# Layer 1's expert blocks in interleaved thirds of their table, and reads of an expert's matrix with a condition

## The chip, the core and the metric

The kernel runs on one core of one Trainium2 chip. The metric is the device time of one execution in microseconds (us); lower is better. A core has a matrix engine (PE, whose weight loads the profile lists apart as PEld), VectorE (DVE), ScalarE (ACT), GpSimd (POOL) and SyncE (SP). Each works through its own instructions in order, and they wait for one another by semaphores. Data moves between the chip's main memory and the on-chip buffers by DMA; in this kernel SP and POOL issue the DMAs.

## The reference, cut to what matters

Four layers follow one another on 2708 rows of 256 numbers. Each adds to its input the result of a graph step (a product with the 2708 x 2708 adjacency matrix, weighted in a different way in each layer) and then that of a feed-forward step. The change touches the feed-forward step of layer 1, in which every row goes to one of eight experts:

```python
H = jax.nn.gelu(xf @ W1 + b1, approximate=False)          # 2708 x 1024
probs = jax.nn.softmax((H @ Wg + bg) / TEMP, axis=-1)     # 2708 x 8
assign = jnp.argmax(probs, axis=-1)
out = jnp.zeros_like(xf)
for e in range(Wd.shape[0]):
    y = H @ Wd[e] + bd[e]                                 # Wd[e] is 1024 x 256
    sel = (assign == e)[:, None]
    out = out + jnp.where(sel, probs[:, e:e + 1] * y, 0.0)
```

## The kernel before, in words

The layers run one after the other, with their edges overlapped. In the feed-forward step of layer 1 the kernel computes H for every row (`hidden`, line 363, called from `send1`, line 1098), writes it to main memory (`hid`), and routes: `route` (line 377) gives every row a place behind the other rows of its expert, and a scatter on POOL (`scatter`, line 502) writes the row's number and its factor to that place in the table `taken`. This is done for three groups of rows (line 30): tiles 0 to 7, 8 to 15 and 16 to 21, a tile being 128 rows.

The experts' products then run by blocks of at most 128 rows of one expert. `blocks` (line 415) works out two tables at run time. The first has NA = 9 blocks that are full after two groups (2048 rows), in order of expert (`full`, line 1325). The second, `rest`, has what remains after all rows are routed, in order of expert too; its first ALWAYS = 15 blocks always run (line 1330), and any further ones stand in a branch (`run_rest`, line 624) that is taken only if there are more. For each block the table says which expert it belongs to (`ei`) and where its rows stand in `taken` (`ix`).

The class `Units` (line 630) does a block in these steps:

- `fetch_names` (line 645): POOL gathers the numbers and factors of the block's rows from `taken` into `names`.
- `fetch_rows` (line 655): POOL gathers the rows of H from `hid` into one of four buffers `hs`, 512 KB.
- `fetch` (line 547): SP loads the block's expert number into a register (`expert_of`, line 530), and `weights1` (line 1052) issues the read of that expert's matrix and bias, 128 rows of 9216 bytes, into one of three buffers `wb`. It waits until the last reader of the buffer, the addition in line 720 three blocks earlier, is done.
- `turn` (line 665): PE transposes the rows (line 670), ScalarE copies them out (line 671).
- the product (line 719): 16 matmul instructions in the profile, into one of two accumulators `yacc`; VectorE adds the bias (line 720) and multiplies by the factor (line 721) into one of two buffers `ys`.
- `scatter` (lines 723 and 505): POOL writes the block's rows to `given` in main memory.

`more` (line 681) keeps names, rows and matrices some blocks ahead. `begin` (line 674) is called in line 1262 with the nine blocks of the first table, before the last group is routed, and `add` (line 690) in line 1332 with the fifteen of the second. `pieces` (line 701) is a generator: its first five steps are taken between parts of the last group's gating in `send1` (lines 1178 to 1189), the others in line 1333. `beside` (line 1206) adds, at blocks given by number, constants of layer 2: the products of line 245 and some small reads on POOL. Layer 2 begins with a read of `given` (line 1406) that waits for every scatter into it. The order of instructions on each engine comes from the compiler's scheduler where it isn't fixed by hand.

Of the kernel before, what the change touches and what calls it, by code (L numbers as in the profile page):

```python
# [8 lines left out]
F32 = mybir.dt.float32  # L9
# [6 lines left out]
P = 128  # L16
N = 2708
D = 256
# [18 lines left out]
def rows(t):  # L37
    return min(P, N - t * P)
# [28 lines left out]
def adj_ffn4(ctx: ExitStack, tc: tile.TileContext, a: dict, out: bass.AP):  # L67
    nc = tc.nc
# [78 lines left out]
    def after(i, past):  # L147

        tc.add_manual_dep(i.ins, past, mybir.DependencyInfo(
            mybir.DependencyClass.NoSync, mybir.DependencyReason.DATA), reason="order")  # L150
# [137 lines left out]
    def spread_out(values):  # L288

        n = values.shape[1]  # L290
        p = ps_tmp()
        for z in range(0, P, Q):
            te.matmul(p[z : z + Q, :n], lhsT=ident[:LAST, :Q], rhs=values[:LAST, :], start=True,
                      stop=True, tile_position=(0, z))
        s.copy(values, p[:, :n])

    def last_rows(dst, parts, filler):

        filler.memset(dst, 1.0)
        for q, k, c0, w in parts:  # L300
            nc.sync.dma_start(dst[q * Q : q * Q + LAST, k : k + w],
                              a["adjT"][FULL * P :, c0 : c0 + w])
# [6 lines left out]
    def by_turns(own):  # L309

        return [(n, t, k) for z in range(2) for n, (t, k, _) in enumerate(own) if n % 2 == z]

    def last_columns(dst):

        v.memset(dst[:, FULL, :], 1.0)
        nc.sync.dma_start(dst[:, :FULL, :], a["adjT"][: FULL * P, N - Q :].rearrange(
            "(t p) c -> p t c", p=P))
        for z in range(0, P, Q):
            nc.sync.dma_start(dst[z : z + LAST, FULL, :], a["adjT"][FULL * P :, N - Q :])
# [445 lines left out]
    taken = [tc.dram_tile([2 * N, XW], F32, name="taken0"), tc.dram_tile([N, 2], F32, name="taken1")]  # L765
# [10 lines left out]
    held = sum(rows(t) for q in GROUPS[:-1] for t in q)  # L776


    NA, MOST = 9, (2 * N + E * (P - 1)) // (2 * P)
# [4 lines left out]
    ALWAYS, HALVES = 13, 2  # L784
    with ExitStack() as l0:
# [15 lines left out]
        hcs, reads, own_rows = [], [], []  # L801
# [87 lines left out]
        for tiles in GROUPS:  # L889
# [8 lines left out]
            for j in range(FULL):  # L898
                r = rows(j)
                ad = gp.tile([P, GMAX * P], F32, name="adrow", bufs=5)[:r, :w]  # L900
                i = nc.sync.dma_start(ad, a["adjT"][j * P : j * P + r, c0 : c0 + w])
# [22 lines left out]
                for p, pair in zip(acc, pairs):  # L924
                    for n in pair:
                        if n == len(own):
                            continue
                        _, k, q = own[n]
# [12 lines left out]
                if end and j == 0:  # L941
                    items = [(early, b, past0, taken[0][: 2 * held0], True) for b in range(N0)]
# [4 lines left out]
                if end and j == NT - 5:  # L947
                    past = list(scattered["taken0"])
# [22 lines left out]
            if tiles is GROUPS[-2]:  # L971
                full = blocks(hw, tp, known, NA - N0, 2 * P, "A", done=early[2], full=True)
        rest = blocks(hw, hc, known, MOST - NA, 2 * P, "B", done=full[2], least=P)
# [9 lines left out]
        past = list(scattered["taken0"])  # L983
        rest = [(rest, b, past, taken[0], False) for b in range(MOST - NA)]
# [37 lines left out]
        for q, t0, t1 in ((P, 0, FULL), (LAST, FULL, NT)):  # L1022
            d = ps_tmp()
            for t in range(t0, t1):
                i = te.matmul(d[:q, t : t + 1], lhsT=cs[:, t * P : t * P + q], rhs=ones,
                              start=(t == t0), stop=(t == t1 - 1))
# [13 lines left out]
    held = sum(rows(t) for q in GROUPS1[:-1] for t in q)  # L1040
    NA, MOST = 9, (N - E) // P + E + 1
    assert NA <= -(-(held - E * (P - 1)) // P)
    ALWAYS = 15
    with ExitStack() as l1:
# [2 lines left out]
        b1 = tp.tile([P, HC], F32, name="b1")  # L1047
        g.dma_start(b1, a["L1_ffn_b1"])
        hw = l1.enter_context(tc.tile_pool(name="h1", side="right", reuse_waits="tile", bufs=1))
        wbs, reads = {}, []  # L1050

        def weights1(b, e):
            wb = wbs["pool"].tile([P, 2048 + D], F32, name="wb", bufs=3)
            i = nc.sync.dma_start(wb, a["L1_ffn_Wdp"][bass.ds(e, 1)].rearrange("e p n -> p (e n)"))
            after(i, reads[-1])
            return wb.rearrange("p (f d) -> p f d", d=D)

# [148 lines left out]
        def beside(b):  # L1206
            if b == NA + 9:
                work1.at_end = scattered["given1"][-1].name
            if b == NA + 4:
# [8 lines left out]
                for i in nc.cur_bb.bb.instructions[first:]:  # L1218
                    if i.engine in (mybir.EngineType.DVE, mybir.EngineType.PE):
                        tc.add_manual_dep(i, work1.last, mybir.DependencyInfo(  # L1220
                            mybir.DependencyClass.NoSync, mybir.DependencyReason.DATA),
                            reason="order")

        work1 = Units(hw, given[1], weights1, hid)
        for tiles in GROUPS1:
            end = tiles is GROUPS1[-1]
# [15 lines left out]
            for j in [*range(12), FULL, *range(12, FULL)]:  # L1242
                r = rows(j)
                if j == FULL:

                    r = P
                    if tiles is GROUPS1[0]:
                        spread_out(sup[:, FULL, :])
                ad = gp.tile([P, 8 * P], F32, name="adrow", tag="adrow", bufs=4)[:r, :w]
                if j < FULL:  # L1250
                    i = nc.sync.dma_start(ad, a["adjT"][j * P : j * P + r, c0 : c0 + w])
                    reads.append(i.ins.name)
                else:
                    last_rows(ad, [(q, 0, c0, w) for q in range(P // Q)], v)
                v.tensor_scalar(mask[:r, j, c0 : c0 + w], ad, 0.0, None, op0=ALU.is_gt)  # L1255
                for t, k, q in own:
                    if t == j:
                        v.tensor_tensor(ad[:, k : k + r], ad[:, k : k + r], ident[:r, :r], ALU.add)  # L1258
                        v.tensor_scalar(diag[:r, j, :r], ad[:, k : k + r], 0.0, None, op0=ALU.is_gt)
                if end and j == NT - 5:  # L1260
                    past = list(scattered["taken1"])
                    work1.begin([(full, b, past, taken[1][:held], True) for b in range(NA)])
                if end and j == 2:
                    cols = gp.tile([P, 8 * P], F32, name="adlast", tag="adrow", bufs=4)[
                        :, : NT * Q].rearrange("p (t c) -> p t c", c=Q)
                    last_columns(cols)
                    v.tensor_scalar(mask[:, :FULL, FULL * P :], cols[:, :FULL, SKIP:], 0.0, None,
                                    op0=ALU.is_gt)
                    own_cols = cols[:, FULL, SKIP:]
                    v.tensor_scalar(mask[:, FULL, FULL * P :], own_cols, 0.0, None, op0=ALU.is_gt)  # L1270
                    v.tensor_tensor(own_cols, own_cols, fold[:, :LAST], ALU.add)
                    v.tensor_scalar(diag[:, FULL, :LAST], own_cols, 0.0, None, op0=ALU.is_gt)
                    last = last_sums(acc[-1].rearrange("p k d -> p (k d)"), cols,
                                     lambda j, r: sup[:r, j, :], D)
                    grow(last[:, None, :], FULL, 1, LAST)
                if j == FULL:
                    for n, t, k in by_turns(own):
                        last_product(acc[n // 2][:, n % 2, :], n // 2, ad, k, sup[:, FULL, :],
                                     False)
                    continue  # L1280
                kept_rows.append((j, ad))
                if end and FULL - 4 < j < FULL - 1:
                    continue
                for p, pair in zip(acc, pairs):
                    for jj, ad in kept_rows:
                        for n in pair:
                            if n == len(own):
                                continue
                            _, k, q = own[n]
                            te.matmul(p[:q, n - pair[0], :], lhsT=ad[:, k : k + q],  # L1290
                                      rhs=sup[:, jj, :], start=(jj == 0 and n == pair[0]),
                                      stop=(jj == FULL - 1 and n == pair[-1]))
                kept_rows.clear()
# [30 lines left out]
            if tiles is GROUPS1[-2]:  # L1324
                full = blocks(hw, gt, known, NA, P, "A", full=True)
        rest = blocks(hw, gt, known, MOST - NA, P, "B", done=full[2])
        too_many = count_left(hw, (rest[2], ALWAYS))
        gate.close()
        past = list(scattered["taken1"])
        items = [(rest, b, past, taken[1], False) for b in range(ALWAYS)]  # L1330
        more = [(rest, b, past, taken[1], False) for b in range(ALWAYS, MOST - NA)]
        work1.add(items)
        for _ in between:
            pass
        work1.run_rest(hc, more, left[0])


# [24 lines left out]
    with tc.tile_pool(name="t3", reuse_waits="tile", bufs=1) as t3:  # L1362
# [34 lines left out]
        with tc.tile_pool(name="g2", reuse_waits="tile", bufs=1) as gp:  # L1397
# [5 lines left out]
            for tiles in FOURS:  # L1403
                n, t0 = len(tiles), tiles[0]
# [3 lines left out]
                for k in range(0, n, 2):  # L1408
                    for q, m in (((P, 2),) if rows(t0 + k + 1) == P else
                                 ((P, 1), (rows(t0 + k + 1), 1))):  # L1410
                        i = k if q == P else k + 1
# [66 lines left out]
            p = ps_tmp()  # L1478
# [7 lines left out]
            for n in (5, 5, 5, 4, 2):  # L1486
# [4 lines left out]
                for j in range(NT):  # L1491
                    r = P
                    e = gp.tile([P, 5 * P], F32, name="e", bufs=4)
                    i = v.scalar_tensor_tensor(e[:r, :w], Rb[:r, c0 : c0 + w], G[:r, j, :],  # L1494
                                           mask[:r, j, c0 : c0 + w], op0=ALU.max, op1=ALU.mult)
# [51 lines left out]
            p = ps_tmp()  # L1547
# [68 lines left out]
        rest = N - len(stretches) * WIDE  # L1616
# [25 lines left out]
        with tc.tile_pool(name="h2", reuse_waits="tile", bufs=2) as hp:  # L1642
# [26 lines left out]
            p = ps_tmp()  # L1669
# [3 lines left out]
            p = ps_tmp()  # L1673
# [86 lines left out]
            was = None  # L1760

            parts = CHUNKS[:-2] + [(CHUNKS[-2][0], 3 * P), (CHUNKS[-2][0] + 3 * P, W + CHUNKS[-1][1] - 3 * P)]
            for c0, w in parts:
                own = tiles_of(c0, w)
                end = c0 + w == N
                hT, i = units(c0, w)
# [17 lines left out]
                was = (own, y)  # L1784
        sums.close()

        with tc.tile_pool(name="g3e", reuse_waits="tile", bufs=1) as ge, ExitStack() as sums:
# [121 lines left out]
            for now, (m, j) in enumerate(slots):  # L1909
# [4 lines left out]
                if j == 0:  # L1914
                    num = pools["psum"].tile([P, 2, W], F32, name="num", bufs=2)
                    den = pools["psum"].tile([P, W], F32, name="den", bufs=2)
                    held = []
# [16 lines left out]
                if j % 2 or j == NT - 1:  # L1934
# [10 lines left out]
                    held = []  # L1945
# [85 lines left out]
```

## Time and profile before

| | |
|---|---|
| median of 3 runs | 1929.87 us (1922.75 to 1935.83) |
| the profiled execution | 1912.16 us |
| its span, first to last instruction | 1910.4 us |
| granted clock of PE, mean | 0.987 |
| PE busy | 1824.7 us (96%) |
| weight loads, VectorE, ScalarE, POOL busy | 1323.7, 1098.8, 642.4, 343.8 us |
| moved by DMA | 243.94 MB |
| reads of `wb` in layer 1 | 24 of 1152 KB each |
| matmuls of line 719 | 384, mean 391 ns, busy 90.7 us |

How to read it: the page divides the span in 40 slices and gives a digit to each engine in each slice, the tenths in which it was busy. A line of a window gives the window, its length, and the busy time and number of instructions of PE, PEld, DVE, ACT and POOL, then the granted clock of PE (1.00 is full), the share of the core's 16 DMA engines that was busy, and GB/s. A line of waits reads "who waited, for whom: us in total, times, the longest". A line of the chain of waits gives the start, the length and the piece of work that the end hung on. `out<-in` names what an instruction writes and reads, and L719 is line 719.

### The profile page before, as it was taken

The numbers are of one execution on the slowest core, as the hardware profiler recorded it, in microseconds if no ns is written. First come the engines' busy times: TensorE is split into PE (matmuls) and PEld (weight loads), VectorE is DVE, ScalarE is ACT, GpSimd is POOL, SyncE is SP. The second block draws the span as 40 slices with busy tenths as digits, with TensorE's granted clock in tenths as the row PEclk, the third lists the DMA queues.
The fourth block names the chain that finished last, engine by engine and source line by source line (L and its number), as shares of the span: only waits on it lengthen the run. The fifth ranks groups of instructions, "written<-read, shape, count | busy, mean of one in ns | idle before, by whom it ended". The sixth has DMA issues, their size and how long they took to land.

```text
span 1910.4 us, 25747 instructions
## 1 busy us (share of the span) xinstructions
PE 1824.7 (96%) x9453; PEld 1323.7 (69%) x9453; DVE 1098.8 (58%) x2498; ACT 642.4 (34%) x1459; POOL 343.8 (18%) x406
## 2 busy tenths in 40 slices
PE   7999999999998999999989799999899999999998
PEld 6888788888887888887778578887566632232344
DVE  6777873443333524454532365555354498999897
ACT  7868752222222303122312232222233551031231
POOL 1004254333321002304356200000000000000000
PEclk9999999999998999999999899999899999999999
DMA  8435657877763453644779610000101000000000
GB/s 273 142 110 156 217 191 287 333 299 294 287 255 127 151 151 101 162 116 121 215 259 360 216 40 1 1 1 1 44 1 34 17 1 23 23 15 26 20 20 16
DMA packets 90141, 243.94 MB, mean 128 GB/s; under 512 B 18159, under 2 KB 44823, under 8 KB 80792
## 3 DMA queue, kind: packets, MB, share of 16 engines
q1 hardware_dynamic: 73048, 199.80, 31.3%
q0 software_dynamic: 16960, 42.42, 6.8%
q8 instruction: 78, 1.28, 0.3%
q14 instruction: 55, 0.45, 0.1%
HBM read 216.29 MB, written 28.71 MB: 128 GB/s over the span
## 4 chain that ended last, share of the span: by engine, by line
PE 40%; DMA 4%; DVE 3%; ACT 2%; issue 1%; POOL 0%; DVEq 0%; POOLq 0%; SPq 0%; ACTq 0%
PE num L1929 10%; PE ps_acc L1502 9%; PE den L1939 6%; PE ps_tmp L367 4%; PE ps_acc L1692 3%; PE ps_tmp L260 2%; PE yacc L719 2%; DMA L_ffn_beta<-in_L_ffn_beta 1%; DMA given<-ys,names 1%; PE ps_acc L260 1%; PE ps_tmp L213 1%; DVE e L1899 1%; DMA names<-taken,b_ix 1%; DMA wb<-in_L_ffn_Wdp 0%; PE ps_acc L670 0%
## 5 line engine op out<-in xcount | busy, mean ns | idle before, releaser
L1899 DVE SCALAR_TENSOR_TENSOR e<-arena,G,mask 128x1024 f32<-128x1024 f32 (+1 forms) x264 | 286.9, 1147 | 13.7 <-PE den L1939 13.6
L1929 PE MATMUL num<-e,wh 128*64 128x512 f32 (+4 forms) x1056 | 215.8, 551 | 0.0
L929 PE MATMUL acc<-msg,wt 128*128 128x256 f32 x882 | 199.0, 382 | 2.8 <-DVE wt L887 1.5
L1502 PE MATMUL ps_acc<-hh,e 128*128 128x257 f32 x882 | 199.3, 382 | 1.9 <-ACT o L1445 1.9
L1290 PE MATMUL acc<-sup,adrow 128*128 128x256 f32 x882 | 198.4, 382 | 0.2 <-DVE adrow L1258 0.2
L929 PEld LDWEIGHTS acc<-msg,wt 128*128 128x128 f32 x882 | 165.5, 191 | 29.4 <-DVE wt L887 2.8
L1290 PEld LDWEIGHTS acc<-sup,adrow 128*128 128x128 f32 x882 | 164.8, 190 | 28.3 <-issue 5.5
L1502 PEld LDWEIGHTS ps_acc<-hh,e 128*128 128x128 f32 x882 | 163.7, 190 | 29.5 <-ACT o L1445 4.5
L583 PE MATMUL ps_acc<-xTs,wa 128*128 128x256 f32 (+1 forms) x768 | 169.4, 373 | 3.5 <-DVE xTs L573 3.4
L617 PE MATMUL yacc<-wb,hTs 128*128 128x256 f32 x736 | 168.4, 380 | 0.0
L585 ACT ACTIVATE hTs<-ps_acc,wa 128x256 f32<-128x256 f32 (+1 forms) x192 | 88.9, 465 | 236.1 <-PE yacc L617 161.9
L583 PEld LDWEIGHTS ps_acc<-xTs,wa 128*128 128x128 f32 x768 | 136.4, 190 | 29.9 <-DVE xTs L573 6.4
L1929 PEld LDWEIGHTS num<-e,wh 128*64 128x64 f32 (+1 forms) x1056 | 66.5, 136 | 127.3 <-issue 105.6
L617 PEld LDWEIGHTS yacc<-wb,hTs 128*128 128x128 f32 x736 | 137.1, 190 | 18.0 <-DVE ys L619 0.6
L1494 DVE SCALAR_TENSOR_TENSOR e<-Rb,G,mask 128x640 f32<-128x640 f32 (+2 forms) x110 | 85.0, 774 | 90.6 <-PE ps_acc L1502 90.4
L1939 PE MATMUL den<-e,wh 128*32 128x512 f32 (+4 forms) x1056 | 118.0, 548 | 0.0
L214 ACT COPY xT<-ps_tmp 128x256 f32<-128x256 f32 x98 | 33.6, 365 | 238.1 <-PE ps_tmp L213 218.9
L1255 DVE TENSOR_SCALAR mask<-adrow 128x1024 uint8<-128x1024 f32 (+1 forms) x66 | 41.1, 624 | 121.1 <-DMA adrow<-in_adjT 120.5
L719 PE MATMUL yacc<-wb,hTs 128*128 128x256 f32 x384 | 90.7, 391 | 12.3 <-DVE ys L720 7.8
L719 PEld LDWEIGHTS yacc<-wb,hTs 128*128 128x128 f32 x384 | 73.1, 195 | 24.1 <-DVE ys L720 8.8
L887 DVE SCALAR_TENSOR_TENSOR wt<-adrow,wt 128x640 f32<-128x640 f32 (+3 forms) x67 | 71.0, 1063 | 28.2 <-ACT wt L141 27.9
L1939 PEld LDWEIGHTS den<-e,wh 128*32 128x32 f32 (+1 forms) x1056 | 30.2, 108 | 77.9 <-issue 73.8
(457 smaller groups left out, 2562.6 us busy)
## 6 DMA issues: line engine op xcount, KB each, us to landing
adhalf<-in_adjT SPq DMA_DIRECT2D x42, 677.0 KB
wb<-in_L_ffn_W2p SPq DMA_DIRECT2D x24, 1152.0 KB
wb<-in_L_ffn_Wdp SPq DMA_DIRECT2D x24, 1152.0 KB
wa<-in_L_ffn_W1b SPq DMA_DIRECT2D x24, 1028.0 KB
adrow<-in_adjT SPq DMA_DIRECT2D x42, 512.0 KB
adrow<-in_adjT SPq DMA_DIRECT2D x42, 320.0 KB
adrow<-in_adjT SPq DMA_DIRECT2D x21, 576.0 KB
adrow<-in_adjT SPq DMA_DIRECT2D x21, 448.0 KB
```

The lines of the kernel that those rows point to most:

```text
L367: te.matmul(p[:, :w], lhsT=w1[:, c, f * P : (f + 1) * P], rhs=xnT[:, c, c0 : c0 + w], start=(c == 0), stop=(c == DC - 1))
L583: i = te.matmul(p[:, f % 2, : m * P], lhsT=w1[:, c, f * P : (f + 1) * P], rhs=xT[:, c, : m * P], start=(c == 0), stop=(c == DC - 1))
L585: s.activation(hT[:, f, : m * P], p[:, f % 2, : m * P], AF.Gelu, bias=bias[:, f : f + 1])
L617: te.matmul(q[:, k, :], lhsT=hT[:, f, k * P : (k + 1) * P], rhs=w2[:, f, :], start=(f == 0), stop=(f == HC - 1))
L719: te.matmul(q, lhsT=hT[:, f, :], rhs=w2[:, f, :], start=(f == 0), stop=(f == HC - 1))
L929: te.matmul(p[:q, n - pair[0], :], lhsT=wt[:, k : k + q], rhs=msg[:r, j, :], start=(j == 0 and n == pair[0]), stop=(j == FULL - 1 and n == ...
L1290: te.matmul(p[:q, n - pair[0], :], lhsT=ad[:, k : k + q], rhs=sup[:, jj, :], start=(jj == 0 and n == pair[0]), stop=(jj == FULL - 1 and n ...
L1494: i = v.scalar_tensor_tensor(e[:r, :w], Rb[:r, c0 : c0 + w], G[:r, j, :], mask[:r, j, c0 : c0 + w], op0=ALU.max, op1=ALU.mult)
L1502: te.matmul(p[:, : D + 1], lhsT=e[:, k : k + q], rhs=hh[:, j, :], start=(j == 0), stop=False)
L1899: v.scalar_tensor_tensor(e[:, :w], slow[:, m % 2, k, :w], G[:, j, 2 * pair + k, :], mask[:, j, c0 : c0 + w], op0=ALU.max, op1=ALU.mult)
L1929: te.matmul(num[k * DK : (k + 1) * DK, hf, :q], lhsT=wh[some, j, 2 * pair + k, :DK], rhs=e[some, h0 - c0 : h0 - c0 + q], start=(j == 0), s ...
L1939: te.matmul(den[z : z + Q, :q], lhsT=wh[some, i, 2 * pair + k, DK : DK + 1] .to_broadcast([some.stop - some.start, Q]), rhs=e[some, h0 - c ...
```

## The change

The blocks of both tables run in another order. `in_thirds(n)` gives the numbers 0, n/3, 2n/3, 1, n/3 + 1, 2n/3 + 1 and so on, so that a buffer, which gets every third block, gets blocks that follow one another in the table. The three buffers are allocated once and kept, with the register of the expert whose matrix each was last asked to hold. The read of a block's matrix has a condition: it is done only if the block's expert isn't the one that the buffer holds. The first read of each buffer has none. Ahead of the branch for further blocks what is remembered is cleared, so that those blocks' reads have no condition at first.

```diff
-        wbs, reads = {}, []
+        wbs, reads = {"held": []}, []
+
+        def in_thirds(n):
+
+            return [k * (n // 3) + i for i in range(n // 3) for k in range(3)]
 
         def weights1(b, e):
-            wb = wbs["pool"].tile([P, 2048 + D], F32, name="wb", bufs=3)
-            i = nc.sync.dma_start(wb, a["L1_ffn_Wdp"][bass.ds(e, 1)].rearrange("e p n -> p (e n)"))
+
+            held = wbs["held"]
+            if len(held) < 3:
+                held.append([wbs["pool"].tile([P, 2048 + D], F32, name="wb", bufs=3), None])
+            wb, was = held[b % 3]
+            held[b % 3][1] = e
+            i = nc.sync.dma_start(wb, a["L1_ffn_Wdp"][bass.ds(e, 1)].rearrange("e p n -> p (e n)"),
+                                  cond=None if was is None else e != was)
             after(i, reads[-1])
             return wb.rearrange("p (f d) -> p f d", d=D)
...
-                    work1.begin([(full, b, past, taken[1][:held], True) for b in range(NA)])
+                    work1.begin([(full, b, past, taken[1][:held], True) for b in in_thirds(NA)])
...
-        items = [(rest, b, past, taken[1], False) for b in range(ALWAYS)]
+        items = [(rest, b, past, taken[1], False) for b in in_thirds(ALWAYS)]
         more = [(rest, b, past, taken[1], False) for b in range(ALWAYS, MOST - NA)]
         work1.add(items)
         for _ in between:
             pass
+        for one in wbs["held"]:
+            one[1] = None
         work1.run_rest(hc, more, left[0])
```

## The prediction

> **What bounds the kernel now.** I read the page's slices first, to find the stage of the change, then the windows over that stage, then who PE waits for in it, then the chain of waits through it, last the instructions of SP and POOL in order of time.
>
> The page, busy tenths in 40 slices of 47.8 us:
>
> ```profile
> PE   7999999999998999999989799999899999999998
> DMA  8435657877763453644779610000101000000000
> ```
>
> PE is nearly full over the whole span (96%), so only the short stretch where it isn't can pay. The matrices of layer 1's experts (`wb`, line 1054) are read from 924.5 to 1069.7 us and used by the matmuls of line 719 from 953.6 us on: slices 20 to 22, where the DMA engines are at 7, 7 and 9 tenths, the densest of the span.
>
> The windows over that stage (length, busy us of PE, PE's weight loads, VectorE, ScalarE, POOL, then clock, DMA share, GB/s):
>
> ```profile
> 953.60:968.20 14.60, 14.60 (x88) 13.25 (x87) 10.12 (x45) 4.00 (x8) 8.90 (x10) 1.00 0.87 285
> 968.20:1007.10 38.90, 29.92 (x147) 25.34 (x146) 7.66 (x26) 6.46 (x13) 23.02 (x24) 0.91 0.79 265
> 1007.10:1078.80 71.70, 66.05 (x350) 56.92 (x348) 15.35 (x40) 16.13 (x29) 39.57 (x42) 1.00 0.89 327
> ```
>
> In 125 us PE is idle 0 + 8.98 + 5.65 = 14.6 us, and in the middle window its clock falls to 0.91. PE's own waits from 968.2 to 1078.8 us (total, times, longest):
>
> ```profile
> PE yacc L719 <- DVE ys L720: 7.8, 3, 5.0
> PE yacc L719 <- DMA wb<-in_L_ffn_Wdp: 4.5, 5, 1.7
> PE ps_acc L670 <- DMA hs<-hid,names: 2.2, 1, 2.2
> ```
>
> Only 4.5 us is a direct wait for a matrix. The 7.8 us are for a free accumulator, and the chain of waits says what holds it:
>
> ```profile
> 973.12 7.61 DMA taken<-names,r_ix
> ...
> 981.52 2.36 DMA names<-taken,b_ix
> ...
> 984.20 5.40 DMA given<-ys,names
> ...
> 990.74 8.51 DMA given<-ys,names
> ...
> 999.80 6.58 PE yacc L719 x16
> 1006.38 0.87 PE ps_acc L670 x8
> 1007.26 3.46 PE yacc L719 x16
> 1010.72 0.87 PE ps_acc L670 x8
> 1011.59 3.46 PE yacc L719 x16
> ```
>
> A block waits because VectorE can't write `ys` (two buffers) before the scatter of two blocks earlier has landed; those scatters wait on POOL, which issues in order, behind a gather that waits for the routing's scatter. The last lines give PE's floor: 3.46 + 0.87 = 4.33 us a block. The block at 999.80 us took 6.58 us, the clock being low after 5.05 us of idleness. So the stage is bound by PE where nothing is late, and by the latency of small DMAs on full DMA engines where something is.
>
> **What the Trainium skill says.** "DMA: Bandwidth & Descriptors", section "Issuing engines are not separate DMA queues": DMAs of SP and POOL run on the same 16 DMA engines and interleave. The trace agrees: POOL's scatters into `given` and `taken` in this stage land 4.0 to 9.9 us after issue, median 6.9, while SP's reads fill the engines. "TensorE: Matmul & The Clock Gate", section "What's actually happening": after an idle window of about 3.4 us the clock falls to half. Trace: 5.05 us idle, then 6.58 us for a block of 3.62. No page bears on a DMA with a condition.
>
> **The change part by part.** I number the blocks of line 719 from 0 to 23 in order of execution; they begin at 953.6, 958.0, 963.9, 968.2 (block 3), 976.3 (4), 983.9 (6), 990.2 (7), 999.8 (8), 1007.1 (9), 1011.4, 1015.8, 1020.1, 1025.4 (13), 1031.1, 1035.4, 1040.0 (16), 1044.9, 1051.0 (18), 1055.4, 1059.8, 1064.2, 1069.7 (22) and 1075.1 (23). Block n uses buffer n mod 3 and its read is issued once VectorE has finished with block n - 3.
>
> *How many reads go.* The reference, evaluated on its own seeded inputs, sends 354, 280, 358, 195, 359, 499, 236 and 427 rows to the eight experts, and 268, 210, 276, 150, 279, 379, 170 and 316 of the first 2048 rows. Whole blocks of 128 in these, the first nine in order of expert: 0 0 1 2 2 3 4 4 5. What remains (98, 152, 102, 67, 103, 371, 236, 427 rows) makes 15 blocks: 0 1 1 2 3 4 5 5 5 6 6 7 7 7 7, just the fifteen that always run. In thirds the experts run 0 2 4, 0 2 4, 1 3 5 and then 0 4 6, 1 5 7, 1 5 7, 2 5 7, 3 6 7. Each column is one buffer, so the reads that fall out are blocks 3, 4, 5, 15, 16, 17, 19, 20 and 23: 9 of 24. A read is 128 rows of 9216 bytes, 1.18 MB: 10.6 MB go of some 44 (24 x 1.18 MB, and 24 x 0.66 MB for the gather and the scatter). Blocks 6 to 14 still need nine reads on end.
>
> *What is added.* On SP a comparison of two registers for 21 reads. SP's register operation in the same place takes 37 ns and its DMA issue 333 ns; a few more such, under 0.2 us a block. SP waits for VectorE 87.8 us in this stage, so that covers it; without that cover it would be 21 x 0.2 = 4.2 us. How long a skipped DMA takes to signal its end the trace doesn't show: at least nothing, at most a real read's. I take little, for both ends lie within the lead of about 8.2 us (from VectorE's end on block n - 3 to block n). The order itself moves no work: the same 24 gathers, 24 scatters and 384 matmuls, each gather and scatter in the same place on POOL. Compute that follows a conditional write may wait for two writers rather than one: 24 x 51 ns, PE's semaphore instruction in line 719, 1.2 us at most, mostly beside waits; I take 0.3 us.
>
> *First gain, blocks 3 to 5.* Their reads are issued at 957.8, 964.8 and 968.4 us; from 960 to 980 us the DMA engines are 99% busy. Without these 3.5 MB, of about 6.6 MB moved then (329 GB/s x 20 us), the gather that PE awaits 2.2 us before block 4 (issued 965.2, landed 975.9, 10.6 us) lands in time at its median of 7.6 us. The routing's scatter (7.61 us in the chain) should come down to between 5.4 us, what the stage's last scatter takes with little else running (issued at 1079.92, SP's read behind it at 1085.35), and 4.0 us, the shortest here: 2.2 to 3.6 us. POOL goes on sooner by as much; I take 2.7 us, up to block 7. Late next is the scatter issued at 990.7 us, 8.5 us long: the reads of blocks 7 and 8 that crowd it are still there, so I leave its stall of 5.05 us and the slow clock (6.58 - 3.62 = 2.96 us) as they are. Gain 2.7 us; bounds 1 and 2.7 + 5.05 + 2.96 = 10.7.
>
> *Second gain, blocks 15 to 23.* From block 9 to 15 all reads remain, so their delays stay (1 us before 13; the product of line 245 after it, 1.14 us of work). Over 4.33 us, the later blocks came late by 0.32 (16), 0.54 (17), 1.77 (18), 0.18 (19 to 21), 1.21 (22) and, block 23 being awaited 1.67 us, 1.7 us. The first three are direct waits for `wb` at full DMA engines: blocks 16 and 17 lose their reads, and 18 keeps one that is issued earlier, since the scatter that held it (7.92 us in the chain) gets free engines. 23 loses its read. Of 22's delay, a wait for the scatter issued behind POOL's constants for layer 2, I take half: 0.6. Sum 0.32 + 0.54 + 1.77 + 0.18 + 0.6 + 1.7 = 5.1 us; bounds 2 and 5.7.
>
> *Sum.* 2.7 + 5.1 - 0.3 = 7.5 us. What follows (last scatter, its landing in 5.4 us, the read of `given`) moves with it. The profiled span is 1910.4 us and its execution 1912.16: after, 1902.9 and 1904.7. The median of the runs shown is 1929.87, 17.7 us above that execution, outside what the change touches: 1922.4.
>
> **The rivals.**
>
> *All stalls go.* If lighter engines also shorten the scatter at 990.7 us, the idle gap stays under what slows the clock, and PE runs at its floor from block 3: 968.2 + 20 x 4.33 + 1.14 = 1056.0 against 1075.1 us, 19.1 us. Time 1910.8. For: each wait ends in a DMA. Against: nine reads on end remain, needing 1.83 MB per 4.33 us, 423 GB/s, above the 396 GB/s of the best 20 us here.
>
> *The reads were hidden.* Direct waits for `wb` are 4.5 us, and POOL, with three issues of about 1.02 us and pauses of 0.3, needs 3.96 us a block of 4.33: it may just take over as the bound. Then 1 to 3 us: 1928. Against: POOL still stays below PE. To this case belongs that fewer reads fall out, which would need a routing other than the reference's: 1930.
>
> *Slower: a condition that holds SP up.* If each of the 21 reads with a condition is issued later by d, on the queue that issues them all in order, nothing happens up to the slack: lead 8.2 us less 5.4 us for a read (an estimate: 1.18 MB at 396 GB/s is 3.0 us, plus 2.4 us, the shortest landing of the small gather of names), 2.8 us. Above this, block by block the excess falls on PE; 19 us are lost, with the gain gone too, at d = 2.8 + (19 + 7.5)/21 = 4.1 us. Time 1949. Nothing in SP's rows is of that size.
>
> **How the numbers follow.** The likely case (4 to 13 us gained) 0.55: its own range is 1917 to 1926. All or most stalls gone 0.17; hidden 0.20; slower 0.08. What can be told from no change is about 1%, 19.3 us, which is the whole of the stage's idle time: so faster by over 1% gets 0.07 (part of the second case, and scatter of the runs shown, 1922.75 to 1935.83), within 1% 0.87, slower by over 1% 0.06. Eight in ten lie from 1908, close under the second case, to 1932, the hidden case with a little cost.
>
> **What would show it.** Right: 15 full reads of `wb` instead of 24 and about 10.6 MB less read from HBM; PE's wait for the gather before block 4 gone; line 719's waits for `wb` down from 4.5 us to about 1; the pace 4.33 us from block 14 on; stage 953.6 to 1078.8 us shorter by 8 us. The stall before block 8 should stay. Wrong: as many bytes as before; SP instructions in line 1054 of over 1 us; POOL waits that grow by what PE's lose; or a difference outside this stage.

## The result, and the profile after

The changed kernel takes 1919.72 us (median of 12 runs, 1916.29 to 1926.75) against 1927.17 us for the kernel before (12 runs, 1920.78 to 1935.83): a ratio of 0.9965 [0.995, 0.9981], or 6.7 us less (3.7 to 9.6). Two later comparisons, each with its own runs of the kernel before on the same chip, gave 0.9984 [0.9972, 0.9996] and 0.9963 [0.995, 0.9977]. None of the intervals reaches 1: the gain is small and real. 7.5 us had been predicted.

The page of the changed kernel, from its profiled execution (1918.45 us, span 1916.7):

```profile
PE   7999998999999999999979799999899999999998
DMA  8435656887773554544758410000101000000000
```

Slices 20 to 22 are at 7, 5 and 8 tenths on the DMA line, where they were at 7, 7 and 9. The page counts 233.33 MB moved, before 243.94: 10.6 MB less, nine reads of 1.18 MB, as worked out. The page's count of bytes read from HBM, 216.29 MB, is the same on both pages, so it doesn't show this; the bytes of the DMA queues do (queue q1: 199.80 MB before, 189.18 after).

The windows over the stage, cut at the same blocks as those of before: to block 3, to block 9, to the last matmul.

```profile
964.80:979.40 14.60, 14.60 (x89) 13.26 (x88) 10.24 (x45) 3.60 (x7) 8.50 (x9) 1.00 0.62 177
979.40:1016.90 37.50, 28.75 (x147) 25.27 (x145) 8.34 (x28) 6.75 (x13) 23.10 (x24) 0.86 0.66 223
1016.90:1084.50 67.60, 65.08 (x350) 56.87 (x348) 14.30 (x39) 16.19 (x29) 39.51 (x42) 1.00 0.68 241
```

The DMA engines are at 0.62 to 0.68 instead of 0.79 to 0.89. The last window is 4.1 us shorter, the middle one only 1.4, at a clock of 0.86. PE's waits from 979.4 to 1084.5 us:

```profile
PE ps_acc L670 <- ACT hTs L671: 8.7, 1, 8.7
PE ps_acc L670 <- issue: 1.4, 1, 1.4
PE yacc L719 <- DMA wb<-in_L_ffn_Wdp: 1.1, 1, 1.1
```

The waits for the gather and for `ys` are gone, and those for a matrix came down from 4.5 to 1.1 us. But there is a wait of 8.7 us that the kernel before did not have. The chain of waits at that place:

```profile
980.81 0.59 ACT hTs L671
981.40 10.99 another core or an unknown queue x2
...
992.40 0.59 ACT hTs L671
...
993.04 1.97 PE ps_acc L670 x8
```

ScalarE waits 11 us for a signal whose sender the trace doesn't name, and VectorE (line 720) waits 8.96 us at the same time; PE's last row before it ends at 984.3 us. From the start of block 3 to that of block 4 it takes 15.4 us. A gap of the same kind (12.5 us there) is in the profiles of two kernels below that take out one read or none, so the change is not its cause. So this profile can't stand alone against the first one of before. In its execution layer 0's expert stage, whose code is the same, is also about 11 us longer (342.3 us, against 331.5). I therefore read the stage from two more profiles without that gap: the kernel before once more, and the changed kernel in its third comparison, both with 330 to 334 us in layer 0. The two are from different chips, so that only differences that the ratios bear out are read from them. Windows of the kernel before, once more:

```profile
967.10:1002.20 35.10, 28.50 (x147) 24.49 (x146) 7.68 (x26) 6.49 (x13) 22.15 (x23) 0.95 0.81 275
1002.20:1073.50 71.30, 65.54 (x350) 56.90 (x348) 15.26 (x40) 16.17 (x29) 40.32 (x43) 1.00 0.91 338
```

and its waits of PE in them:

```profile
PE yacc L719 <- DMA wb<-in_L_ffn_Wdp: 3.8, 4, 2.5
PE yacc L719 <- DVE ys L720: 3.6, 2, 2.9
PE ps_acc L670 <- DMA hs<-hid,names: 3.0, 1, 3.0
```

The changed kernel, third comparison:

```profile
966.70:1001.30 34.60, 27.14 (x147) 23.30 (x145) 7.69 (x26) 7.42 (x14) 21.94 (x22) 1.00 0.71 224
1001.30:1070.00 68.70, 65.39 (x348) 57.05 (x348) 15.34 (x41) 15.24 (x27) 40.56 (x44) 1.00 0.70 246
```

and its waits:

```profile
PE yacc L719 <- DVE ys L720: 6.5, 3, 3.2
PE yacc L719 <- DMA wb<-in_L_ffn_Wdp: 3.6, 4, 1.6
PE ps_tmp L245 <- DVE w_l L270: 0.6, 1, 0.6
```

The wait for the gather is gone here too. The waits for `ys` are not, and those for a matrix are as long as before. What went is seen best from the blocks' starts. This table has the time from the start of one block to that of another, in us, read from the timelines (the last column is an experiment told below):

| blocks | before | before, once more | after, third | only 3 reads left |
|---|---|---|---|---|
| 0 to 4 | 22.7 | 23.5 | 20.4 | 18.9 |
| 4 to 9 | 30.8 | 26.2 | 28.8 | 21.6 |
| 9 to 14 | 24.0 | 26.2 | 26.3 | 22.6 |
| 14 to 23 | 44.1 | 41.4 | 38.7 | 38.1 |
| 0 to 23 | 121.5 | 117.3 | 114.1 | 101.2 |

The first and last stretches are those whose reads fell out (3 to 5, 15 to 17, 19, 20, 23), and there the time is gained. Between blocks 4 and 14, where nine reads on end remain, nothing is. There the DMA engines are busy for 0.85 of the time in the third comparison, much as before (0.84 and 0.87); from block 14 to 23 their share falls from 0.90 and 0.93 to 0.60.

That the stage is shorter does not hang on these three profiles alone. From block 0 to 23 the five profiles here of kernels with 23 or 24 reads take 117.3 to 121.7 us (mean 119.9), the seven with 15 reads and the same two buffers `ys` 113.0 to 116.1 (mean 114.4), the gap of the first included, and the one with three reads 101.2.

### The profile page after: what moved, and what is told of

It reads as the page before. It is cut to its first block, busy times and chain, and to the rows that moved or that the text cites. A ratio compares the mean times of both kernels' runs of the same rounds, so it can differ in the third digit from the quotient of the medians.

```text
span 1916.7 us, 25790 instructions
## 1 busy us (share of the span) xinstructions
PE 1826.6 (95%) x9453; PEld 1326.0 (69%) x9453; DVE 1097.8 (57%) x2498; ACT 642.8 (34%) x1459; POOL 344.1 (18%) x406
## 2 busy tenths in 40 slices
DMA packets 88846, 233.33 MB, mean 122 GB/s; under 512 B 18015, under 2 KB 44679, under 8 KB 80648
## 3 DMA queue, kind: packets, MB, share of 16 engines
q1 hardware_dynamic: 71752, 189.18, 29.9%
HBM read 216.29 MB, written 28.71 MB: 128 GB/s over the span
## 4 chain that ended last, share of the span: by engine, by line
PE 42%; DVE 2%; DMA 2%; ACT 2%; issue 1%; another core or an unknown queue 1%; POOL 0%; SPq 0%; POOLq 0%; DVEq 0%; ACTq 0%
PE num L1941 10%; PE ps_acc L1514 9%; PE den L1951 6%; PE ps_tmp L367 4%; PE ps_acc L1704 3%; PE yacc L719 3%; PE ps_tmp L260 2%; DMA L_ffn_beta<-in_L_ffn_beta 1%; PE ps_acc L670 1%; PE ps_acc L260 1%; PE ps_tmp L213 1%; DVE e L1911 1%; DVE e L1506 0%; ACT wh L1843 0%
## 5 line engine op out<-in xcount | busy, mean ns | idle before, releaser
L617 PEld LDWEIGHTS yacc<-wb,hTs 128*128 128x128 f32 x736 | 138.3, 192 | 25.3 <-issue 3.8
L1506 DVE SCALAR_TENSOR_TENSOR e<-Rb,G,mask 128x640 f32<-128x640 f32 (+2 forms) x110 | 85.1, 774 | 90.5 <-PE ps_acc L1514 90.4
L1265 DVE TENSOR_SCALAR mask<-adrow 128x1024 uint8<-128x1024 f32 (+1 forms) x66 | 41.4, 627 | 123.2 <-DMA adrow<-in_adjT 122.8
L887 DVE SCALAR_TENSOR_TENSOR wt<-adrow,wt 128x640 f32<-128x640 f32 (+3 forms) x67 | 71.1, 1063 | 27.5 <-ACT wt L141 19.8
L619 DVE TENSOR_TENSOR ys<-yacc,wb 128x256 f32<-128x256 f32 x46 | 19.5, 424 | 112.7 <-PE yacc L617 103.4
```

Source lines behind the costliest of these rows:

```text
L617: te.matmul(q[:, k, :], lhsT=hT[:, f, k * P : (k + 1) * P], rhs=w2[:, f, :], start=(f == 0), stop=(f == HC - 1))
```

## The experiments

The theory to be tested: the gain is that of fewer bytes on the DMA engines. The rivals: it is that of the new order; the condition itself costs or gains something; and, formed on the way, PE does its work in another order.

**One part alone.** The order without the condition (24 reads), and the condition without the order (the table's own order, so that of the reads only block 23's falls out). The first diff is against the kernel before, the second against the changed one:

```diff
-                    work1.begin([(full, b, past, taken[1][:held], True) for b in range(NA)])
+                    work1.begin([(full, b, past, taken[1][:held], True) for b in in_thirds(NA)])
...
-        items = [(rest, b, past, taken[1], False) for b in range(ALWAYS)]
+        items = [(rest, b, past, taken[1], False) for b in in_thirds(ALWAYS)]
```

```diff
-                    work1.begin([(full, b, past, taken[1][:held], True) for b in in_thirds(NA)])
+                    work1.begin([(full, b, past, taken[1][:held], True) for b in range(NA)])
...
-        items = [(rest, b, past, taken[1], False) for b in in_thirds(ALWAYS)]
+        items = [(rest, b, past, taken[1], False) for b in range(ALWAYS)]
```

> The blocks in thirds, but every block's matrix is read (24 reads, no condition). My theory: the order moves no work, so 0.9985 to 1.0015. Rival (the gain comes from the order, by other gathers and scatters side by side): 0.9965, like the change.

> The reads with a condition, but the blocks in the order of before, so that only the read of block 23 falls out (23 reads of 24). My theory: SP's few extra register operations are covered and block 23's wait of 1.7 us goes, 0.998 to 1.0005. Rival (a condition costs, on SP or by later ends of skipped reads): over 1.002.

Measured beside 1922.86 us for the kernel before: order alone 1922.42, ratio 1.0001 [0.9987, 1.0016]; condition alone 1925.58, 1.001 [0.9994, 1.0026]. Neither part shows a gain by itself. Only together do they take nine reads out, and only together do they gain. The order as a cause is out, and so is that the three buffers are allocated once, which the condition alone has too.

**The change again, and the same reads left out without a condition.** In the second kernel the nine reads are struck out when the program is built, so SP has no comparison and no skipped instruction. That is right for this routing alone: with another, blocks would use a wrong matrix.

```diff
-            i = nc.sync.dma_start(wb, a["L1_ffn_Wdp"][bass.ds(e, 1)].rearrange("e p n -> p (e n)"),
-                                  cond=None if was is None else e != was)
-            after(i, reads[-1])
+            if b not in (3, 4, 5, 15, 16, 17, 19, 20, 23):
+                i = nc.sync.dma_start(wb, a["L1_ffn_Wdp"][bass.ds(e, 1)].rearrange("e p n -> p (e n)"))
+                after(i, reads[-1])
```

> The changed kernel as it is, for a second profile and a second ratio. My theory (fewer bytes shorten what PE waits for): ratio to before 0.995 to 0.998; in the profile block 4 begins about 13.5 us after block 1 (2.7 us sooner than in the first profile of before), and the 10 us gap that stood ahead of block 4 in the first profile of after is chance of that execution. Rival (the change makes a new wait there): block 4 begins some 25 us after block 1 again, with ScalarE and VectorE both waiting for PE.

> As the change, but the nine reads that fall out for this input are left out when the kernel is built, and the other fifteen have no condition; it computes the reference for this routing only. My theory: a skipped read costs next to nothing, so the ratio to before is that of the change within 0.0015. Rival (the condition, or the end of a skipped read, costs some us): lower than the change by 0.002 or more.

Beside the same 1922.86 us: the change 1918.86, 0.9984 [0.9972, 0.9996]; struck out 1914.61, 0.9954 [0.9941, 0.9967]. With the same 15 reads, the kernel without conditions is 0.003 lower in its ratio; its median is 4.3 us lower. In its trace PE also does its work in another order: it alternates 8 transposes and a block's 16 matmuls, where the others do the transposes of 2.5 blocks (20) ahead of the products of blocks 4 and 5. That could be these 4 us, so I tested it.

**PE's order held.** Each transpose and each matmul of line 719 is made to follow the one before it in program order, so that PE alternates throughout, in the changed kernel and in the kernel before:

```diff
+            self.on_pe = None
...
-                    te.transpose(p[:, i * P : (i + 1) * P], h[:, (f + i) * P : (f + i + 1) * P], ident)
+                    self.next_on_pe(te.transpose(p[:, i * P : (i + 1) * P],
+                                                 h[:, (f + i) * P : (f + i + 1) * P], ident))
...
+        def next_on_pe(self, i):
+
+            if self.on_pe is not None:
+                after(i, self.on_pe)
+            self.on_pe = i.ins.name
...
-                    te.matmul(q, lhsT=hT[:, f, :], rhs=w2[:, f, :], start=(f == 0), stop=(f == HC - 1))
+                    self.next_on_pe(te.matmul(q, lhsT=hT[:, f, :], rhs=w2[:, f, :], start=(f == 0),
+                                              stop=(f == HC - 1)))
```

> The change with its conditions, and PE held to the order transpose, product, transpose, product in all 24 blocks; the scheduler had put the transposes of two and a half blocks ahead of the products of blocks 4 and 5 in before, in the change and in all runs so far but static_skip. New theory (static_skip gained more than the change by that other order on PE, and a condition or a skipped read costs nothing): the ratio of static_skip, 0.9954, within 0.0015. Rival (a skipped read's condition or its end costs 5 us): 0.998, as the change.

> The kernel before with PE held to the same alternating order. If order and bytes add up: the order is worth what after_pe_order gains on the change, some 0.003, so 0.997. Rival (the order pays only when the reads are gone): 0.9985 to 1.0015.

Beside 1909.79 us: the changed kernel in this order 1902.13, 0.9956 [0.9942, 0.997]; the kernel before in this order 1910.19, 0.9993 [0.9982, 1.0004]. For the kernel before no gain by the order shows. The kernel before was run once more in the same comparison, for the profile read above:

> The kernel before, unchanged, for a second profile. Theory: its first profile (1912.16 us, 15 us below its median) was a quick execution; the second has the expert stage of layer 0 at some 341 us, as all later profiles, instead of 331.5, and block 4 some 12 us after block 3, as order_only and cond_only, instead of 8.1. Rival: it repeats the first profile, and the gap before block 4 comes with the change.

That one execution took 1907.06 us, inside the range of the others on that chip (1905.59 to 1918.4). Its stage differs from the first profile's, 117.3 us against 121.5 from block 0 to 23: so much lies between two executions of one kernel.

In another comparison, beside 1911.5 us, the changed kernel was run with and without it:

> The change as it is, beside the three that follow on the same chip. My theory: 0.996 to 0.998 (0.9965 and 0.9984 were measured on two chips), 1.5 to 4 us above after_pe_order_2. Rival (PE's order is worth nothing): within 1.5 us of it.

> The change with PE held to transpose, product, transpose, product, as after_pe_order. Expected 0.9945 to 0.9965; its place between after_third and static_skip_2 splits the price of PE's order from that of the conditions.

1905.41, 0.9963 [0.995, 0.9977], without it, and 1903.29, 0.9964 [0.9943, 0.9985], with it: no difference shows. The theory that PE's order explains the difference has fallen. No kernel here that serves every routing is measurably faster than the change.

> Nine reads left out when the kernel is built, no conditions, as static_skip; PE's order is that of after_pe_order_2. If a condition and a skipped read cost nothing: within 2 us of after_pe_order_2. If they cost some us: 3 us or more below it.

Struck out once more, beside the same 1911.5 us: 1899.73, 0.9931 [0.9909, 0.9954], again 0.003 under the change, its median 5.7 us lower. The two intervals just overlap here; in the first comparison they did not. The row of all matmuls of line 719 (times are those of the first and last start) has little of it. The changed kernel, third comparison:

```profile
L719 PE MATMUL yacc<-wb,hTs x384: 378/379/483, 952.2 to 1069.5; 128*128 128x256 f32 x192
```

and struck out, the same chip:

```profile
L719 PE MATMUL yacc<-wb,hTs x384: 378/379/631, 949.7 to 1065.9; 128*128 128x256 f32 x192
```

117.3 and 116.2 us: 1.1 us in the stage. Of the 3.7 us between the spans of these two executions 2.5 lie ahead of block 0. But there two executions with conditions on this chip differ by as much as 2.0 us (952.2 and, with PE's order held, 950.2), so that a single pair does not place the difference. On SP, the changed kernel's rows for the reads (minimum, median, maximum in ns, then first and last start):

```profile
L1063 SPq ALU_OP  x42: 37/38/54, 947.3 to 1054.2; - x42
L1063 SPq DMA_DIRECT2D wb<-in_L_ffn_Wdp x24: 73/333/374, 923.3 to 1060.9; - x24
```

Two more register operations of 38 ns, and a third of 50 ns rather than 37, for each of 21 reads make 1.9 us in the stage, and nine skipped reads take 73 to 102 ns rather than 333, 2.1 to 2.3 us less. So the 4 to 6 us do not show in the length of SP's instructions. Where they are stays open. The condition alone (21 conditions, one read skipped) cost between -1.2 and 5.0 us by its interval, which neither shows nor excludes it.

**A third buffer for `ys`.** The waits for `ys` that remain would come from its two buffers being held by scatters that land late. The edit is made to the changed kernel with PE's order held.

```diff
-                y = pool.tile([P, D], F32, name="ys", bufs=2)
+                y = pool.tile([P, D], F32, name="ys", bufs=3)
```

> As after_pe_order, with three buffers ys in place of two, so that VectorE waits for the scatter of three blocks before. My theory (what is left of the stalls in blocks 4 to 8 is the landing of scatters that hold ys): 2 to 5 us below after_pe_order, 0.993 to 0.9945. Rival (they are POOL's wait for the routing's scatter, which ys doesn't touch): within 0.0015 of after_pe_order.

1902.30 us, 0.9953 [0.9937, 0.997], against 1902.13 with two buffers, both beside 1909.79. Its one profile has no wait of PE for `ys` left and the matmuls of the stage in 110.4 us rather than 117.4, but seven us do not appear in the median. A single profile is no measurement of the time: the 2 to 5 us expected did not show, and a gain too small for these runs is not excluded.

**Only three reads.** In the changed kernel with PE's order held, all but the first read of each buffer are left out, without a condition, so that blocks from 3 on multiply with another expert's matrix. The work of PE, ScalarE, VectorE and POOL is the same; 12 more reads (14.2 MB) are gone.

```diff
-            i = nc.sync.dma_start(wb, a["L1_ffn_Wdp"][bass.ds(e, 1)].rearrange("e p n -> p (e n)"),
-                                  cond=None if was is None else e != was)
-            after(i, reads[-1])
+            if b < 3:
+                i = nc.sync.dma_start(wb, a["L1_ffn_Wdp"][bass.ds(e, 1)].rearrange("e p n -> p (e n)"))
+                after(i, reads[-1])
```

> As after_pe_order_2, but only the first three of the 24 matrices are read and all blocks use them (the other 21 reads are left out, so the values aren't the reference's). My theory (the gain is the bytes, and what reads remain still cost): 3 to 8 us below after_pe_order_2, PE at 4.33 us a block from block 9 on, and the stalls of blocks 5 to 8 that hang on the routing's scatter and on ys left. Rival (the remaining stalls are POOL's and the scatters' alone): within 2 us of after_pe_order_2.

1889.55 us beside 1911.5, 0.9883 [0.9858, 0.9907]: 13.7 us under the changed kernel with PE's order held, where 3 to 8 had been expected. I had expected the stalls of blocks 5 to 8, which hang on POOL and its scatters, to remain. They did not. Its windows from block 3 on:

```profile
968.60:994.60 26.00, 26.00 (x147) 23.23 (x146) 7.80 (x26) 6.47 (x13) 20.00 (x20) 1.00 0.35 107
994.60:1059.00 64.40, 64.38 (x351) 56.94 (x349) 15.48 (x40) 16.24 (x29) 42.51 (x45) 1.00 0.40 120
```

and the start of its chain (the matmuls of line 719 are its line 727):

```profile
968.89 3.46 PE yacc L727 x16
972.34 0.87 PE ps_acc L671 x8
973.22 3.46 PE yacc L727 x16
```

PE is busy in all but 0.02 of 90.4 us; no block waits for anything, and each takes 3.46 + 0.87 us. The waits for a matrix go by construction. Those for `ys` and for the routing's scatter go too, though POOL has the same work: so these waits come with the other 12 reads. How the reads cause them is seen in part in the landing of POOL's scatters into `given`. There are 24, but the trace gives the landing of only 7, 16 and 9 of them, in the kernel before once more, the changed one (third comparison) and the one with three reads. In this order, the median us from issue to landing:

```profile
given<-ys,names POOLq DMA_INDIRECT x24, 6.3
```

```profile
given<-ys,names POOLq DMA_INDIRECT x24, 4.0
```

```profile
given<-ys,names POOLq DMA_INDIRECT x24, 2.5
```

The longest are 7.9, 9.4 and 4.2 us. The ends are clear: 6.3 to 7.3 in three profiles with all reads, 2.5 with three. Those with 15 reads lie anywhere between, with medians of 3.9 to 6.6 in five profiles with the engines 0.70 to 0.78 busy, so that no landing can be told from the load alone. The routing's scatter also lands sooner with three reads: POOL's gather from `taken`, which in the third comparison is held 5.2 us for it, starts 3.9 us after it was issued and is not held.

This fits what the Trainium skill states ("DMA: Bandwidth & Descriptors", section "Issuing engines are not separate DMA queues"): transfers of SP and of POOL share the 16 engines. The share of busy time there, in the windows from block 3 on, is 0.81 and 0.91 in the kernel before once more, 0.71 and 0.70 in the changed one, 0.35 and 0.40 with three reads. That the queueing of the small transfers behind the reads is what delays them is argued from this, not shown apart. Against the kernel with nine reads struck out, which has no condition either (PE's order made no difference that showed above), these 12 reads are worth 0.9931 - 0.9883 = 0.0048, or 9.2 us; in the two profiles the stage to block 23 is 11.8 us shorter (113.0 to 101.2).

## Why the prediction held, point by point

- **Nine reads, 10.6 MB less.** Right: in the third comparison line 1063 has 15 instructions of 332 to 374 ns and nine of 73 to 102 ns, the short ones at blocks 3, 4, 5, 15, 16, 17, 19, 20 and 23, and 10.6 MB less went over the queues.
- **First gain, 2.7 us.** Its first half held: the wait for the gather before block 4, 2.2 and 3.0 us in two profiles of before, is gone, and block 4 begins 2.3 to 3.1 us sooner. Its second half failed at the step that shortens the routing's scatter: it was to fall from 7.61 us to between 4.0 and 5.4. In the chain of the third comparison it didn't:

```profile
971.66 7.99 DMA taken<-names,r_ix
...
983.14 4.21 DMA given<-ys,names
```

  It takes 7.99 us, and 8.33 in the kernel before once more. It is issued 19.5 us after block 0 starts, in the kernel before as well, and lands no sooner, so POOL isn't sooner either, and block 7 begins 35.7 us after block 0, before 36.6 and 36.1: 0.3 to 0.8 us, not 2.7. Block 4 came sooner, but the blocks behind it wait for POOL as before. The kernel before with PE's order held shows the same: with all 24 reads its block 4 begins 20.1 us after block 0, and the stage is no shorter for it (121.7 us).
- **What is late next.** Right in kind: the stalls at blocks 6 to 9 stay. From block 4 to 14 the changed kernel takes 55.1 us, the kernel before 54.7 and 52.4, and 44.2 without the other reads. That the clock stays low there did not hold in every profile: 0.91 and 0.95 before, 1.00 in the third comparison, 0.86 in the first with its other gap. Nor does the length of a wait alone decide it. A block after 2.88 us of idleness in the kernel before once more, less than the 3.4 us that the prediction quotes, took 5.41 us; one after 3.24 us in the third comparison took 3.72:

```profile
996.12 5.41 PE L719 MATMUL yacc<-wb,hTs 128*128 128x256 f32 x16 [2.88 <-DVE ys L720]
```

```profile
995.75 3.72 PE L719 MATMUL yacc<-wb,hTs 128*128 128x256 f32 x16 [3.24 <-DVE ys L720]
```

- **Second gain, 5.1 us.** The pace came as said: from block 14 to 20 each takes 4.33 us, and 14 to 23 takes 38.7 us where the kernel with three reads takes 38.1. Against the execution that the sum was made for this is 5.4 us. But the kernel before once more needs 41.4 us there, 2.7 more than the changed kernel: blocks 16 to 18 were late in the first profile by 2.6 us, and in the second not at all. I had taken one execution's delays for the kernel's.
- **Cost of the condition, 0.3 us.** Too small, or something else is in it: two comparisons put the change 4 to 6 us above the same reads without it. SP's own rows agree with the prediction. Waits for a matrix of about 1 us were foretold: 1.1 in the first profile, 3.6 in the third.
- **The sum.** 7.5 us predicted; 6.7, 3.1 and 7.1 measured. From block 0 to 23 the two profiles of before have 121.5 and 117.3 us, mean 119.4, the third comparison 114.1: 5.3. So the path was right, fewer bytes and fewer waits at the two ends of the stage, but the closeness of the time is in part luck. The terms were mis-sized (0.3 to 0.8 at block 7 for 2.7; 2.7 to 5.4 for 5.1), and errors in both directions met: the reads struck out without a condition gained 8.8 and 13.2 us, more than the 7.8 of the two gains, and the change lost 4 to 6 of this to something that no term has. Outside the stage the profiles show no steady difference: from the start of the last matmul of line 719 to the end all fourteen take 832.0 to 833.8 us, and ahead of block 0 single executions differ by some us whatever the kernel.
- **The rivals.** That all stalls go is what happens when the other 12 reads go as well: 101.2 us from block 0 to 23, where the prediction's starts gave 1056.0 - 953.6 = 102.4. The argument against it, nine reads on end, fits the blocks 4 to 14, where the engines stayed as busy as before. (The 1%, 19.3 us, that the prediction calls the stage's idle time is more than that, which is 14.6; it is near the 19.1 of this rival, with the slow clock in it.) That POOL takes over as the bound is refuted by the same kernel. That the condition holds SP up is not seen on SP; whether the 4 to 6 us are a cost of it is not shown.

## What to carry to other kernels

A read that is seldom waited for can still be worth removing: look at what else uses the DMA engines in that window; here it was small scatters and gathers that came late. But here the gain came only where the bytes went; where the same density of reads remained next door, work that arrived sooner waited there. And take delays of single blocks from two executions before adding them up.

## What the runs showed of the hardware

- A read whose condition is false costs SP 73 to 102 ns rather than 333 and moves nothing; its comparison costs two operations of 38 ns. The whole change still runs 4 to 6 us above the same kernel without conditions, twice; the cause is open.
- The landing of a small scatter is longer under load: medians of 6.3 to 7.3 us with all reads (engines 0.79 to 0.91 busy), 2.5 with three (0.35 to 0.40). Between, at 0.70 to 0.78, five profiles with 15 reads have 3.9 to 6.6.
- After a wait of PE of 2.88 us the next block of 16 matmuls took 5.41 us, after one of 3.24 us in another profile 3.72.
- The same code differs between the profiles of different chips by more than this change: layer 0's expert stage takes 330 to 334 us in the profiles of two chips and 341 to 343 in those of a third and in the first of the changed kernel. In these last there are also 12.5 to 16.7 us from the start of block 3 to that of block 4, where 4.33 us is the floor (9.4 us from block 4 to 5 with the reads struck out). Its cause is open.
